# A subject-dependent matrix product with residual: two rows of a sample per partition, and the array in four 64x64 tiles

## The chip, the cores and the metric

The kernel runs on one core of a Trainium2 chip. A core has a matrix engine (TensorE, PE in the profile, with its weight loads as PEld), a vector engine (VectorE, DVE), a scalar engine (ScalarE, ACT), GpSimd (POOL) and SyncE (SP). Here ACT and SP only issue transfers and POOL mostly waits on semaphores for the others. Transfers between the device memory (DRAM) and the on-chip memory (SBUF, 128 partitions) run on 16 DMA engines. Products land in PSUM, which has 128 partitions with 8 banks of 512 fp32 numbers each.

The metric is the time of one execution on the device in microseconds (us), lower is better.

## The reference

For each of 128 samples there is a subject number between 0 and 7, and each subject has a 128x128 matrix. The output is the input plus the matrix of the sample's subject, transposed, times the sample:

```python
# x: (128, 128, 1024) fp32, subjects: (128,) int32, weights: (8, 128, 128) fp32
w = weights[subjects]
out = x + jnp.einsum('bct,bcd->bdt', x, w)
```

So 67.11 MB are read, 67.11 MB are written and 0.52 MB of weights are read. Everything is fp32.

## The kernel before

A sample is a matrix of 128 rows (c) by 1024 columns (t). One row lies in one partition: the 1024 numbers of row c, 4 KB, in partition c. Four samples make a slot (2 MB), and SBUF holds twelve slots in `x_all`. There are 32 slots of work (NT), which run through the twelve places in turn.

- ACT issues all loads, one DMA per sample (`load`, through the helper `transfer` at L67). The DRAM side is given as 32 runs of four rows (16 KB), the SBUF side as 128 partitions of 4 KB. From slot 12 on it waits until the place's previous occupant has been stored. Slot 11 waits until the weights are sorted (`s_sort`), because they pass through its place first.
- POOL waits for each slot's landing and passes it on to TensorE (`s_ready`).
- VectorE reads the subject numbers of a slot into registers and copies the four matrices out of `w_all` (`place`, L165) into the small tiles w0 to w3. A signal `s_go` tells TensorE.
- TensorE multiplies (`multiply`, L174): a slot goes in two halves of two samples. Each sample takes two products of a 128x128 matrix with 128x512 columns. The two halves use the two PSUM tensors ps0 and ps1, of four banks each.
- VectorE adds (`add`, L186): it reads a half of 2048 columns from PSUM, adds the input and writes the sum over the input in `x_all`.
- SP stores a slot when its sums are done (`store`, L67). Between slots 8 and 23 it holds stores back until four more slots are done (EARLY, LAST, BEHIND). The last twelve slots are stored two at a time (4 MB), the others singly (2 MB).

At the start the weights come with one DMA on SP's queue (L192). VectorE sorts them into `w_all` with two transposes (L208, L227) and copies (L230), POOL doing four of sixteen copies. TensorE runs three products of zeros (L200) to wake its clock.

The order on each engine is the order of the code. TensorE's and VectorE's parts are loops with one turn per slot; the lists of ACT, SP and POOL are written out in full. The engines meet only through semaphores.

Of the kernel before, what the change touches and what calls it, by code (L numbers as in the profile page):

```python
# [30 lines left out]
G = 2  # L31
H = 2

N = 512

SLOTS = 12

P_SLOTS = 2

BEHIND = 4  # L40
# [4 lines left out]
PAIR = 2  # L45
WHOLE = 6

DMA = 16

SORTED = 18  # L50

IDLE = 3
# [28 lines left out]
def kernel(  # L81
# [10 lines left out]
    NT = B // (G * H)  # L92
# [4 lines left out]

    room = -(nc.sbuf_base + -nc.sbuf_base % 32) % ALIGN
    if room:
        sbuf("room", C, room // 4)  # L100
    x_all = sbuf("x_all", C, SLOTS * H * G * T)
    xs = [
        x_all[:, i * H * G * T : (i + 1) * H * G * T].rearrange("c (q t) -> c q t", t=T)
        for i in range(SLOTS)
    ]
    w_all = sbuf("w_all", C, S, D)
    w_raw, w_mid, w_late = (xs[SLOTS - 1][:, q, :] for q in range(3))
    ws = [sbuf(f"w{i}", C, 1, D) for i in range(H * G)]
    zeros = sbuf("zeros", C, N)
    given, near, wrap = (sbuf(name, 1, B, dtype=I32) for name in ("given", "near", "wrap"))  # L110
    index = sbuf("index", 1, B + H * G, dtype=I32)
    ps = [
        ctx.enter_context(nc.psum_tensor(f"ps{i}", [D, G, T], F32)).ap() for i in range(P_SLOTS)
    ]

    s_given = tc.alloc_semaphore("s_given")
    s_wall = tc.alloc_semaphore("s_wall")
    s_index = tc.alloc_semaphore("s_index")
    s_zeros = tc.alloc_semaphore("s_zeros")
    s_product = tc.alloc_semaphore("s_product")  # L120
    s_added = tc.alloc_semaphore("s_added")

    s_ready = tc.alloc_semaphore("s_ready")
    s_go = tc.alloc_semaphore("s_go")

    s_slot = [tc.alloc_semaphore(f"s_slot{k}") for k in range(SLOTS)]
    s_head = tc.alloc_semaphore("s_head")
    s_sort = tc.alloc_semaphore("s_sort")

    def emptied(i):  # L130
        turns = i // SLOTS
        return DMA * (H * G + 1) * turns - (DMA * G if i >= SLOTS and i % SLOTS == 0 else 0)

    def load(engine, i, q):
        transfer(
            nc,
            engine,
            xs[i % SLOTS][:, q, :],
            x[i * H * G + q].rearrange("(a r) t -> a (r t)", r=ROWS),
        ).then_inc(s_head if i * H * G + q < G else s_slot[i % SLOTS], DMA)  # L140

    def store(i, n):
        at = i % SLOTS * H * G * T
# [19 lines left out]
    def place(h, subject):  # L163
        for q in range(h * G, (h + 1) * G):
            copy = nc.vector.tensor_copy(ws[q], w_all[:, bass.ds(subject[q], 1), :])  # L165
        copy.then_inc(s_go, 1)
# [143 lines left out]
```

## Time and profile before

| what | value |
|---|---|
| time, median of 3 runs | 322.95 us (322.77 to 322.99) |
| span of the profiled execution, first to last instruction | 320.9 us |
| TensorE matmul busy | 248.9 us (78%) |
| VectorE busy | 172.6 us (54%) |
| bytes moved | 134.76 MB, mean 420 GB/s |
| mean granted TensorE clock | 0.893 of full |

The median of the runs stands 2.05 us above the profiled execution's span: the time of a run also has what lies before the first and behind the last instruction. The profile is of one such execution; no separate run time is given for it.

How to read it: the page cuts the span into 40 equal slices of 8.0 us, and a digit is the busy share of a slice in tenths. In a row of a group, after the bar, stand the busy time in us, the mean duration of one instruction in ns, the idle time of the engine just before them and what ended most of it. A row of a stretch (a:b) has its length, the busy us of PE, PEld, DVE and POOL with the count of instructions, the granted clock, the busy share of the DMA engines and GB/s. A row of the timeline has start, duration (us), engine, line, operation and, in brackets, the idle time before it. A row of a queue has its packets, its MB and its share of the 16 engines' time. The rows of the DMA issues have the size of one and the median time from issue to landing.

### The profile page before, as it was taken

What the parts mean: (1) busy time and instruction counts of PE and PEld (TensorE: products, weight loads), DVE (VectorE), ACT (ScalarE), POOL (GpSimd) and SP (SyncE); (2) the same over time, 40 slices, a digit from 0 to 9 for tenths busy, and PEclk for the clock granted to TensorE, in tenths of its full rate; (3) what the DMA queues carried; (4) which work ended last, traced back from release to release, by engine and by line L of the source; (5) the groups of instructions that cost most, each with busy time, mean ns of one, the idle gap of its engine ahead of it and who ended that gap; (6) DMA issues with size and microseconds to landing.
All of it is one profiled execution on the core that took longest, in us unless ns stands there. A gap on an engine that the chain in (4) does not pass through costs nothing. (4 is left out here: it accounts for less than half of the span.)

```text
span 320.9 us, 2386 instructions
## 1 busy us (share of the span) xinstructions
PE 248.9 (78%) x518; PEld 102.8 (32%) x518; DVE 172.6 (54%) x216; POOL 1.9 (1%) x8
## 2 busy tenths in 40 slices
PE   6199999999997699998498469988599957874000
PEld 2134444444433244443133224333244422331000
DVE  4636776777676167775435362675367745066000
POOL 0200000000000000000000000000000000000000
PEclk9679999999999599999789797999799989599555
DMA  7999999999999999999999999999999999999996
GB/s 294 425 425 412 426 423 432 429 423 425 425 425 425 425 424 425 425 429 425 429 435 431 427 427 429 425 425 425 425 425 425 425 425 425 427 427 455 429 445 274
DMA packets 10803, 134.76 MB, mean 420 GB/s; under 512 B 2481, under 2 KB 2482, under 8 KB 3122
## 3 DMA queue, kind: packets, MB, share of 16 engines
q1 hardware_dynamic: 4658, 67.64, 49.7%
q10 hardware_dynamic: 6144, 67.12, 49.6%
q14 instruction: 1, 0.01, 0.0%
HBM read 67.63 MB, written 67.11 MB: 420 GB/s over the span
## 5 line engine op out<-in xcount | busy, mean ns | idle before, releaser
L174 PE MATMUL ps<-x_all,w 128*128 x512 | 243.8, 635 | 42.0 <-PEq L170 34.3
L186 DVE TENSOR_TENSOR x_all<-ps,x_all 128x2048 f32 x64 | 146.7, 2292 | 117.3 <-DVEq L185 117.3
L174 PEld LDWEIGHTS ps<-x_all,w 128*128 128x128 f32 x512 | 100.9, 203 | 185.2 <-issue 184.6
L165 DVE COPY w<-w_all 128x128 f32 x132 | 23.2, 219 | 0.8 <-DVE w_all L230 0.8
L200 PE MATMUL ps<-zeros 128*128 128x512 f32 x6 | 5.2, 1033 | 1.7 <-DVE zeros L197 1.7
L230 DVE COPY w_all<-x_all 32x256 f32<-32x256 f32 x12 | 3.9, 326 | 0.4
L208 DVE STREAM_TRANSPOSE x_all<-x_all 128x1024 f32<-128x1024 f32 x1 | 2.0, 1992 | 3.1 <-DMA x_all<-in_L_cond_weights_dram 3.1
L200 PEld LDWEIGHTS ps<-zeros 128*128 128x128 f32 x6 | 1.8, 328 | 3.7 <-issue 2.1
L230 POOL COPY w_all<-x_all 32x256 f32<-32x256 f32 x4 | 1.7, 425 | 8.3 <-DVE x_all L227 8.1
L227 DVE STREAM_TRANSPOSE x_all<-x_all 128x1024 f32<-128x1024 f32 x1 | 1.2, 1225 | 0.0
L197 DVE MEMSET zeros<- 128x512 f32 x1 | 0.5, 485 | 1.0 <-SPq L190 1.0
L217 DVE CUSTOM_DVE_ANT_0 index<-near,wrap 1x256 uint16<-1x256 uint16 x1 | 0.3, 280 | 0.0
L215 DVE TENSOR_SCALAR wrap<-near 1x128 int32<-1x128 int32 x1 | 0.2, 215 | 0.0
L213 DVE TENSOR_SCALAR near<-given 1x128 int32<-1x128 int32 x1 | 0.2, 205 | 0.0
L297 POOL MEMSET const-bfloat16-1.0<- 128x1 bf16 x1 | 0.1, 100 | 0.0
L297 POOL MEMSET const-float32-0.0<- 128x1 f32 x1 | 0.1, 98 | 0.2 <-issue 0.2
L297 POOL MEMSET const-uint8-127<- 128x1 uint8 x1 | 0.1, 98 | 0.0
L297 POOL MEMSET const-float32-1.0<- 128x1 f32 x1 | 0.1, 97 | 0.0
L297 DVE BASE_LOAD x1 | 0.0, 21 | 0.1
L211 DVE MEMSET index<- 1x4 int32 x1 | 0.1, 62 | 0.0
## 6 DMA issues: line engine op xcount, KB each, us to landing
x_all<-in_x_dram ACTq DMA_DIRECT2D x128, 512.0 KB, 34.2
out_dram<-x_all SPq DMA_DIRECT2D x20, 2048.0 KB, 18.3
out_dram<-x_all SPq DMA_DIRECT2D x6, 4096.0 KB, 30.3
x_all<-in_L_cond_weights_dram SPq DMA_DIRECT2D x1, 512.0 KB, 3.7
given<-in_itok_B_dram SPq DMA_DIRECT2D x1, 0.5 KB
```

Of the source, the lines that this page charges most:

```text
L165: copy = nc.vector.tensor_copy(ws[q], w_all[:, bass.ds(subject[q], 1), :])
L174: mm = nc.tensor.matmul(ps[h][:, q % G, t : t + N], ws[q][:, 0, :], x_all[:, bass.ds(at, N)], start=True, stop=True,)
L186: nc.vector.tensor_tensor(mine, ps[h].rearrange("d g t -> d (g t)"), mine, ALU.add).then_inc(s_added, 1)
L197: nc.vector.memset(zeros, 0.0).then_inc(s_zeros, 1)
L200: nc.tensor.matmul(ps[P_SLOTS - 1][:, G - 1, :N], zeros[:, :D], zeros, start=True, stop=True)
L208: nc.vector.transpose(w_mid.rearrange("p (e h w j) -> p j h e w", e=S, h=4, w=4), w_raw).then_inc(s_sort, 1)
L213: nc.vector.tensor_scalar(near, given, -S, S - 1, ALU.max, ALU.min).then_inc(s_index, 1)
L215: nc.vector.tensor_scalar(wrap, near, 0, S, ALU.is_lt, ALU.mult).then_inc(s_index, 1)
L217: nc.vector.tensor_tensor(index[:, :B], near, wrap, ALU.add).then_inc(s_index, 1)
L227: nc.vector.transpose(w_late, w_mid).then_inc(s_sort, 1)
L230: engine.tensor_copy(w_all[32 * v : 32 * (v + 1), 2 * o : 2 * (o + 1), :], w_late[32 * o : 32 * (o + 1)].rearrange("c (e v d) -> c v e d", ...
L297: nc = _bacc.Bacc("TRN2", target_bir_lowering=False, num_devices=1)
```

## The change

The layout. A partition now holds two consecutive rows of a sample, 8 KB in one piece, so a sample fills 64 partitions and two samples lie above each other. A slot is still four samples: two pairs, p = 0 from the first half of the batch and p = 1 from the second half (FAR = 64 samples further on). In a pair, h = 0 is the sample in the lower 64 partitions and h = 1 the one in the upper. Inputs and outputs have places of their own: `x_in` for four slots, `x_out` for eight.

The product. The 128 rows of a sample are two rows (r) in each of 64 partitions, and so are the 128 rows of the result (e). So a sample's matrix is cut into four 64x64 pieces (r, e), and a product of 512 columns takes two matmuls (r = 0, 1) that add up in PSUM. Each uses a quarter of the array: rows by h, columns by the output's side. For p = 0 the output lies on the side of the input; for p = 1 it changes sides (`h ^ p`). The four products (p, h) that follow each other in the code use the four different quarters.

The upper sample of p = 1 is multiplied one slot after the slot in which it was loaded (`i - p * h`). With that, the two outputs of p = 1 in a slot are neighbours in the batch, in the order in which they lie, and one DMA of 128 partitions stores the slot. The last sample of the batch is loaded early and fills the gap in slot 0.

The residual. VectorE no longer adds the input: `place` adds the identity (`same`, made by POOL) to the matrix while copying it, so the product is already the sum. VectorE copies PSUM to `x_out` in pieces of 1024 columns. A slot fills all of PSUM in two halves of two banks in each tensor; `s_free` gives a half back to TensorE after its copies. The small weight tiles are double (w00, w01 and w10, w11), filled two slots ahead.

The queues. ACT's list, before and after; 64x8x256 are the weights, 64x2048 a single sample:

```order
L67 DMA x_all<-in_x_dram 128x1024 x44
L67 DMA x_all<-in_x_dram 128x1024 [waits s_sort]
L67 DMA x_all<-in_x_dram 128x1024 x3
L67 DMA x_all<-in_x_dram 128x1024 [waits s_slot0]
L67 DMA x_all<-in_x_dram 128x1024 x3
L67 DMA x_all<-in_x_dram 128x1024 [waits s_slot1]
```

```order
L65 DMA x_out<-in_L_cond_weights_dram 64x8x256
L65 DMA x_in<-in_x_dram 128x2048 x2
L65 DMA x_in<-in_x_dram 64x2048
L65 DMA x_in<-in_x_dram 128x2048 x5
L65 DMA x_in<-in_x_dram 128x2048 [waits s_eaten] x56
L65 DMA x_in<-in_x_dram 64x2048 [waits s_eaten]
```

The weights stand ahead of the samples now, a load is two samples, and the first load that waits is the eighth of two samples where it was the forty-fifth of one.

TensorE's turn of the loop, before (one slot; ps0 and ps1 are the halves of PSUM, w0 to w3 the matrices of the four samples):

```order
L174 ISA [waits s_go,s_ready]
L174 MATMUL ps0<-x_all,w0 128x512
L174 ISA
L174 MATMUL ps0<-x_all,w0 128x512
L174 ISA
L174 MATMUL ps0<-x_all,w1 128x512
```

and after, the first half of a slot (there are four slots in a turn now; the quarters are not shown, w00 belongs to p = 0 and w01 to p = 1):

```order
L210 MATMUL ps0<-x_in,w00 64x512 [waits s_go,s_ready,s_free]
L210 MATMUL ps0<-x_in,w00 64x512
L210 MATMUL ps1<-x_in,w01 64x512 x2
L210 MATMUL ps0<-x_in,w00 64x512 x2
L210 MATMUL ps1<-x_in,w01 64x512 x2
L210 MATMUL ps0<-x_in,w00 64x512 [waits s_free]
```

Eight products of the whole array have become 32 of a quarter, without register work between them, and TensorE waits for a half of PSUM twice per slot.

VectorE's turn, before (half a turn):

```order
L154 TENSOR_LOAD index
L186 ISA [waits s_product]
L186 TENSOR_TENSOR x_all<-ps0,x_all 128x2048
L165 ISA
L165 COPY w0<-w_all 128x128
L165 ISA
L165 COPY w1<-w_all 128x128
```

and after (one slot but for the last three of its four weight tiles):

```order
L222 ISA [waits s_room,s_product]
L222 COPY x_out<-ps0 128x1024
L222 ISA
L222 COPY x_out<-ps1 128x1024
L222 ISA [waits s_product]
L222 COPY x_out<-ps0 128x1024
L222 ISA
L222 COPY x_out<-ps1 128x1024
L186 ISA
L186 TENSOR_TENSOR w00<-w_all,same 64x256
```

The two adds per slot have become four copies, and the plain copies of weights have become adds with the identity.

The core of the diff:

```diff
-SLOTS = 12
-P_SLOTS = 2
-BEHIND = 4
+IN = 4
+OUT = 8
+BEHIND = 3
-IDLE = 3
+IDLE = 8
...
     def load(i, p, first, n):
+        at = (i % IN * P + p) * SIZE
+        low = first % H * A
+        return transfer(
             nc,
+            nc.scalar,
+            x_in[low : low + n * A, at : at + SIZE],
+            x[first : first + n].rearrange("h (b r) t -> (h b) (r t)", r=ROWS),
+        )
...
     def store(i):
+        at = i % OUT * P * SIZE
+        rows = out.rearrange("b (a r) t -> (b a) (r t)", r=R)
+        (step, _), last = rows.ap
         return transfer(
             nc,
             nc.sync,
+            bass.AP(
+                tensor=rows.tensor,
+                offset=rows.offset + H * i * A * step,
+                ap=[[step, C], [(FAR - 1) * A * step, P], last],
+            ),
+            x_out[:, at : at + P * SIZE].rearrange("a (o f) -> a o f", o=1),
+        )
...
-    def place(h, subject):
-        for q in range(h * G, (h + 1) * G):
-            copy = nc.vector.tensor_copy(ws[q], w_all[:, bass.ds(subject[q], 1), :])
-        copy.then_inc(s_go, 1)
+    def place(u, subject):
+        return [
+            nc.vector.tensor_tensor(
+                ws[u][p][h * A : (h + 1) * A],
+                w_all[h * A : (h + 1) * A, bass.ds(subject[p * H + (h ^ p)], 1), :],
+                same[h * A : (h + 1) * A],
+                ALU.add,
+            )
+            for p in range(P)
+            for h in range(H)
+        ]
...
+    def multiply(i):
         nc.tensor.wait_ge(s_go, 1).then_inc(s_go, -1)
         nc.tensor.wait_ge(s_ready, 1).then_inc(s_ready, -1)
+        for b in range(BANKS):
+            if b < BANKS // 2:
+                nc.tensor.wait_ge(s_free, 1).then_inc(s_free, -1)
+            for r in range(R):
+                for p in range(P):
+                    for h in range(H):
+                        bank = b * 2 % BANKS + (b * 2 // BANKS + h) % 2
+                        e, t = divmod(bank * N, T)
+                        rows = slice(h * A, (h + 1) * A)
+                        cols = slice((h ^ p) * A, ((h ^ p) + 1) * A)
+                        at = ((i - p * h) % IN * P + p) * SIZE + r * T + t
+                        mm = nc.tensor.matmul(
+                            ps[p][cols, bank],
+                            ws[i % 2][p][rows, 0, r * D + e * A : r * D + (e + 1) * A],
+                            x_in[rows, at : at + N],
+                            start=r == 0,
+                            stop=r == R - 1,
+                        )
+            if b >= BANKS // 2:
+                mm.then_inc(s_product, 1)
+
+    def copy(slot, p, half):
+        at = slot * (P * SIZE) + (p * SIZE + half * T)
+        return nc.vector.tensor_copy(
+            x_out[:, bass.ds(at, T)],
+            ps[p][:, half * (T // N) : (half + 1) * (T // N)].rearrange("d b n -> d (b n)"),
+        )
+
+    def sort(h):
+        nc.vector.tensor_copy(
+            w_all[h * A : (h + 1) * A].rearrange("c s (r e a) -> c (s r) e a", r=R, e=R),
+            w_raw.rearrange("c (g a e) -> c g e a", a=D // R, e=R),
+        ).then_inc(s_sort, 1)
...
+        for i in range(NT):
+            for p in range(P):
+                if i >= IN - p:
+                    nc.scalar.wait_ge(s_eaten, i - IN + 1 + p)
+                n = H if (i, p) != (NT - 1, 1) else 1
+                load(i, p, p * FAR + i * H, n).then_inc(s_in[i % IN], DMA)
+            if i == 0:
+                load(IN - 1, 1, B - 1, 1).then_inc(s_head, DMA)
...
+        nc.gpsimd.wait_ge(s_head, DMA)
         for i in range(NT):
+            if i >= OUT:
+                nc.gpsimd.wait_ge(s_out[i % OUT], stored(i - OUT)).then_inc(s_room, 1)
+            nc.gpsimd.wait_ge(s_in[i % IN], DMA * P * (i // IN + 1)).then_inc(s_ready, 1)
+
+        for i in range(NT - 1):
+            nc.sync.wait_ge(s_added, i + 1 + (BEHIND if EARLY <= i < NT - LAST else 0))
...
+        with nc.vector.Fori(0, NT // 2) as turn:
+            for u in range(2):
+                subject = subjects_of(bass.ds(turn * (2 * Q) + (u + 2) * Q, Q))
+                slot = (turn * 2 + u) % OUT
+                nc.vector.wait_ge(s_room, 1).then_inc(s_room, -1)
+                for half in range(2):
+                    nc.vector.wait_ge(s_product, 1).then_inc(s_product, -1)
+                    for p in range(P):
+                        copied = copy(slot, p, half)
+                        if half and not p:
+                            copied.then_inc(s_eaten, 1)
+                    copied.then_inc(s_free, 1)
+                placed = place(u, subject)
+                placed[0].then_inc(s_added, 1)
+                placed[-1].then_inc(s_go, 1)
+        with nc.tensor.Fori(0, NT // IN):
+            for i in range(IN):
+                multiply(i)
```

204 lines of the change are left out of this document (93 added, 111 removed).

## The prediction, made before the changed kernel ran

> **What bounds the kernel now.** I read the page from the top: span, busy shares, the 40 slices, the DMA queues.
>
> ```profile
> span 320.9 us, 2386 instructions
> PE 248.9 (78%) x518; PEld 102.8 (32%) x518; DVE 172.6 (54%) x216; POOL 1.9 (1%) x8
> PEclk9679999999999599999789797999799989599555
> DMA  7999999999999999999999999999999999999996
> GB/s 294 425 425 412 426 423 432 429 423 425 425 425 425 425 424 425 425 429 425 429 435 431 427 427 429 425 425 425 425 425 425 425 425 425 427 427 455 429 445 274
> DMA packets 10803, 134.76 MB, mean 420 GB/s; under 512 B 2481, under 2 KB 2482, under 8 KB 3122
> q1 hardware_dynamic: 4658, 67.64, 49.7%
> q10 hardware_dynamic: 6144, 67.12, 49.6%
> ```
>
> No compute engine is above 78%, while the DMA row stands at 9 in 38 of 40 slices and the two queues fill 99.3% of the 16 engines' time. Then I asked for long stretches, so that the edges of large transfers matter little.
>
> ```profile
> 10.00:30.00 20.00, 15.46 (x30) 6.56 (x31) 9.96 (x20) 0.40 (x1) 0.75 1.02 430
> 70.00:118.00 48.00, 42.98 (x92) 17.91 (x92) 29.15 (x34) 0.00 (x0) 0.93 1.01 426
> 133.00:240.00 107.00, 86.21 (x179) 35.64 (x178) 57.00 (x69) 0.00 (x0) 0.92 1.01 426
> 297.00:319.00 22.00, 0.00 (x0) 0.00 (x0) 0.00 (x0) 0.00 (x0) 0.50 0.96 410
> ```
>
> The rate is 426 GB/s, whatever PE does beside it, also in the last 22 us, where only stores run. 134.76 MB at 426 GB/s is 316.3 us, and 4.6 us are left for the first and last slice. So the bound is the transfers. The waits say the same from the other side: VectorE waits for products, and TensorE, in its longest waits (L170 waits for a slot's landing), for data.
>
> ```profile
> DVE x_all L186 <- DVEq L185: 117.3, 64, 8.3
> PE ps L174 <- PEq L170: 34.3, 12, 4.6
> ```
>
> Early on the loads are far ahead, and there the compute shows its own pace. This is VectorE's timeline, one add in two:
>
> ```profile
> 24.63 2.29 DVE L186 TENSOR_TENSOR x_all<-ps,x_all 128x2048 f32 x1 [0.80 <-DVEq L185]
> ...
> 31.69 2.29 DVE L186 TENSOR_TENSOR x_all<-ps,x_all 128x2048 f32 x1 [0.80 <-DVEq L185]
> ...
> 38.74 2.29 DVE L186 TENSOR_TENSOR x_all<-ps,x_all 128x2048 f32 x1 [0.81 <-DVEq L185]
> ```
>
> A slot of four samples takes 7.05 us of compute, and 4.19 MB at 426 GB/s is 9.85 us of transfer. The slack is 2.8 us per slot; the change spends most of it.
>
> The runs' median of 322.95 us is 2.05 us above this execution's span; I carry these 2.05 us over unchanged.
>
> **TensorE, per slot.** The line of the product, and two rows of its weight loads, at half and at full clock:
>
> ```profile
> L174 PEld LDWEIGHTS ps<-x_all,w x512: 186/190/338, 14.5 to 291.6; 128*128 128x128 f32 x171
> L174 PE MATMUL ps<-x_all,w x512: 592/592/1217, 14.5 to 292.0; 128*128 x171
> L174 PEldq FUSED_REGOPS  x256: 46/46/103, 14.4 to 287.3; - x128
> 109.02 0.34 PEld L174 LDWEIGHTS ps<-x_all,w 128*128 128x128 f32 x1 [0.52 <-issue]
> 113.60 0.19 PEld L174 LDWEIGHTS ps<-x_all,w 128*128 128x128 f32 x1 [0.24 <-issue]
> ```
>
> 256 products of the program are 512 matmuls, each with its own weight load: an fp32 product is two instructions. At full clock one follows another every 0.19 + 0.24 = 0.43 us, at half clock every 0.86; a slot is 16 x 0.43 = 6.9 us. After the change a slot has 32 products, 64 instructions, still of 512 columns. If four run at once, 64 / 4 x 0.43 = 6.9 us, as before; if two, 13.8; if none, 27.5. No row shows a quarter of the array at work, so these are the bounds. I take four: the four products that stand next to each other differ in rows or columns of the array, and each pair of r and bank fills it. This choice decides the forecast.
>
> The weight loads, 64 per slot with 64 columns instead of 16 with 128, lie beside the matmuls now. If their time goes with the columns it is 64 x 0.095 = 6.1 us and stays under 6.9; if a load costs 0.19 whatever its width, 12.2 us.
>
> **VectorE, per slot.**
>
> ```profile
> L186 DVE TENSOR_TENSOR x_all<-ps,x_all 128x2048 f32 x64 | 146.7, 2292 | 117.3 <-DVEq L185 117.3
> L165 DVE COPY w<-w_all 128x128 f32 x132 | 23.2, 219 | 0.8 <-DVE w_all L230 0.8
> L230 DVE COPY w_all<-x_all 32x256 f32<-32x256 f32 x12 | 3.9, 326 | 0.4
> L227 DVE STREAM_TRANSPOSE x_all<-x_all 128x1024 f32<-128x1024 f32 x1 | 1.2, 1225 | 0.0
> ```
>
> Removed are two adds (4.6 us) and four copies of weights (0.9). Added are four copies of 1024 columns out of PSUM and four adds of the identity, 64x256. Between 128 columns (219 ns) and 2048 (2292) one column costs 1.08 ns, so a copy is 1.19 us (upper end 1.23, the row of 1024 columns), and an adding of 256 columns 0.36 us (0.33 to 0.45). Together 4.8 + 1.4 = 6.2 us, against 5.5 before.
>
> **The ring of the two.** All of PSUM now belongs to one slot, in two halves. From the end of the third quarter of the matmuls, VectorE copies half 0 (2.4 us, beside the fourth quarter of 1.7) and then half 1 (2.4); only then may the next slot's second quarter start, and two quarters (3.45) bring it to the same point: 8.3 us, with three handoffs 8.3 to 8.8. I take 8.5: above the old 7.05, below the 9.85 of transfer. What hides it is the transfer; from 11.3 us (below) 32 slots and some 10 us for the last copies and store fit into 320 us up to 9.3 us per slot.
>
> **The transfers.** Bytes are the same, and packets of 16 KB too. The loads go from 128 to 65 DMAs, the stores from 26 to 34. q10 with 6144 packets took 49.6 / 67.12 = 0.739% per MB, q1 with fewer packets per MB 0.735%; by that difference (0.2 engine-us per MB for 23 packets) a small packet costs about 9 ns, and 55 fewer DMAs of 16 such packets save 880 x 9 / 16 = 0.5 us. In SBUF and on the way out the contiguous piece is 8 KB instead of 4 KB, 16384 fewer pieces. Their price stands in no row: at least 0, at most that of a packet, 9 ns, which is 9.4 us. The nearest rows are the rates: 426 in the long stretches, 430 over 10 to 30 us. I take 430 as reachable, 134.76 MB x (1/0.426 - 1/0.430) = 2.9 us less; ends 0 and 6.5 (435, the highest slice before 250 us).
>
> The Trainium skill, DMA: Bandwidth & Descriptors (section Why small descriptors are slow), puts a fixed 3 cycles of 32 bytes on each piece, under a ceiling of 435 GB/s: as an estimate, 128/131 of it is 425 GB/s for 4 KB, which the slices agree with, and 256/259 is 430 for 8 KB; by it the sum would lose 3.7 us here.
>
> **The start.** Before:
>
> ```profile
> L200 PE MATMUL ps<-zeros 128*128 128x512 f32 x6 | 5.2, 1033 | 1.7 <-DVE zeros L197 1.7
> x_all<-in_L_cond_weights_dram SPq DMA_DIRECT2D x1, 512.0 KB, 3.7
> 0.90 23.58 ACTq L67 DMA_DIRECT2D x_all<-in_x_dram  x31
> 8.52 4.26 DVE L230 COPY w_all<-x_all 32x256 f32<-32x256 f32 x12
> 13.63 0.63 DVE L165 COPY w<-w_all 128x128 f32 x4 [0.85 <-DVE w_all L230]
> 14.54 9.84 PE L174 MATMUL ps<-x_all,w 128*128 x16 [7.71 <-DVE w L165]
> ```
>
> Both transposes and sixteen sorting copies go; two copies of 2048 columns come (1.8 us each, by 0.84 ns per column between the rows of 128 and 256). Weights at about 5, register load 0.85, sorting 3.7, placing 1.5: 11 us. The sixteen warm-up instructions end there too (six at 0.86 from 1.7, the rest at 0.43: 11.1). So the first slot starts near 11.3 instead of 14.5, and frees its input after 6.9 of matmul and the third copy, at 20.2. But only four input slots exist where twelve did: without a freed slot ACT can issue 8.4 MB, and from 2.5 us (what the first slice lacks) at 426 GB/s these last until 22.2. ACT's wait on a freed slot holds all later loads behind it. Cover: 2 us, about what a transfer needs to get going (the weights' 3.7 less 1.2 of moving). I charge 0.5 us; ends 0 and 4. The weights move from SP's queue to the head of ACT's, so the first samples come 0.52 MB / 426 GB/s = 1.2 us later; no byte is added, and 11.3 already has them. Their 1 KB pieces, 384 more at 9 ns on 16 engines, add 0.2. POOL's new wait (a slot is ready only when the store of eight slots earlier has landed) holds TensorE back; a store is issued three slots after its sum, so it has four slots, 34 us at 8.5, to land, against a median of 18.3 us for the same 2 MB before:
>
> ```profile
> out_dram<-x_all SPq DMA_DIRECT2D x20, 2048.0 KB, 18.3
> ```
>
> I cost it at nothing; a landing above 34 us would make it part of the starved case. The end costs nothing either: three slots of stores are held back (BEHIND) and one is under way, 4 x 4.9 us of transfer, longer than the 11 us that the last slot needs after its load.
>
> **Sum:** 322.95 - 0.5 - 2.9 + 0.2 + 0.5 = 320.2 us.
>
> **Rivals.**
> *Two at once (slower).* Place: TensorE's queue. The two instructions of one product want the same quarter of the array. If a matmul may not start before the one ahead of it in the program has, the second holds up the other three products, and the pattern settles at two at work: 13.8 us per slot. It decides from 9.3 us per slot, or 0.58 us for each four. Time: 11.3 + 32 x 13.8 + 10 + 2 = 465 us. For it: the two-for-one rows above; against: nothing measured. The Trainium skill, TensorE: Matmul & The Clock Gate (section Part 3), states that matmuls begin and end in program order and only weight loads are pulled ahead; no run here shows it for quarters yet.
> *Another limit on TensorE (slower).* Weight loads of 0.19 in a row: 11.3 + 32 x 12.2 + 12 = 414 us; or quarters not overlapping at all, about 900.
> *Starved (slower).* The ring at 9.6 instead of 8.5, or the start's gap at its far end with stores held back from slot 8 on while four input slots are full: 11.3 + 32 x 9.6 + 12 = 331; 324 to 340.
> *No faster pieces (the same).* The rate stays 426: 322.95 - 0.5 + 0.2 + 0.5 = 323.2.
>
> **Chances.** What a measurement of this kernel can tell from no change is about 0.2%, 0.65 us. Forecast 0.42, two at once 0.30, another TensorE limit 0.12, starved 0.10, the same 0.06. So faster 0.42, same 0.06, slower 0.52: the likeliest single case is faster, though the slower ones together weigh more. Its own range is 316.5 (rate 435, the rest unchanged) to 322.3. For 8 in 10 the range must take in the two-at-once case: 316.5 to 470.
>
> **What would show it.** Right: the slices at 428 to 431 GB/s in long stretches, matmuls of four quarters starting within a fraction of 0.43 us, VectorE's copies at 1.2 us, first product near 11.3, no slice near 22 us below 9. Two at once: PE at 9 in every slice, full clock throughout, DMA near 300 GB/s, and matmul starts in pairs each 0.43 us. Starved: DMA digits of 7 or 8 between 20 and 120 us. Wrong altogether, if PSUM copies take well over 1.23 us or the identity's adding over 0.45, for then the ring passes 9.3 without TensorE.

## The result, and the profile after

The changed kernel takes 338.05 us (median of four runs, 336.89 to 341.25) beside 322.86 us for the kernel before on the same chip: a ratio of 1.049, 95% interval 1.044 to 1.054. The prediction was 320.2 us, faster. It is 15 us slower. All times below are medians of undisturbed runs; one run of the kernel with half of the products, 332.36 us at a lower granted clock, is not counted.

This is the page of the changed kernel: the span, the busy times, the 40 slices (8.4 us each now) and the transfers.

```profile
span 336.2 us, 5241 instructions
PE 251.0 (75%) x2064; PEld 93.3 (28%) x2064; DVE 209.0 (62%) x275; POOL 1.0 (0%) x6
DMA  7998999999999968999999999999999999999993
GB/s 224 368 404 273 354 417 431 433 433 427 429 431 431 413 277 281 433 429 429 429 433 431 431 429 427 433 431 429 431 427 429 431 431 431 428 400 427 429 433 157
DMA packets 10440, 134.81 MB, mean 401 GB/s; under 512 B 1602, under 2 KB 2115, under 8 KB 2115
```

TensorE is as busy as before (251.0 against 248.9 us), although it now runs 2048 matmul instructions of a quarter of the array each. Away from the holes most slices move 427 to 433 GB/s, where before most moved 425; there are 879 fewer packets under 512 B. Most of the time is lost in three holes of the GB/s row: the first five slices (0 to 4), slices 14 and 15 (277 and 281), and the last one, 39 (157). The same by stretches (GB/s is the last column):

```profile
0.00:10.00 10.00, 8.33 (x13) 3.56 (x14) 4.47 (x12) 1.05 (x6) 1.00 0.77 261
10.00:20.00 10.00, 6.93 (x44) 2.44 (x46) 3.00 (x8) 0.00 (x0) 0.83 1.00 370
14.00:17.00 3.00, 2.48 (x12) 0.88 (x16) 0.00 (x0) 0.00 (x0) 0.50 0.97 415
20.00:30.00 10.00, 8.54 (x80) 3.08 (x76) 6.30 (x8) 0.00 (x0) 1.00 0.84 334
25.00:26.00 1.00, 1.00 (x12) 0.16 (x4) 1.00 (x2) 0.00 (x0) 1.00 0.04 16
30.00:50.00 20.00, 16.39 (x147) 5.68 (x136) 14.71 (x18) 0.00 (x0) 1.00 0.99 367
70.00:100.00 30.00, 22.14 (x200) 8.63 (x204) 20.61 (x29) 0.00 (x0) 1.00 1.01 431
100.00:150.00 50.00, 41.01 (x367) 15.07 (x359) 32.71 (x42) 0.00 (x0) 1.00 0.92 377
150.00:200.00 50.00, 39.78 (x344) 14.52 (x344) 36.58 (x48) 0.00 (x0) 0.98 1.01 430
320.00:336.00 16.00, 0.00 (x0) 0.00 (x0) 2.36 (x5) 0.00 (x0) 0.53 0.69 293
```

and the answering stretches of the kernel before:

```profile
0.00:10.00 10.00, 5.16 (x6) 1.85 (x6) 5.60 (x12) 1.50 (x7) 0.99 0.80 315
30.00:50.00 20.00, 20.00 (x47) 8.41 (x46) 14.20 (x19) 0.00 (x0) 1.00 1.00 415
310.00:320.90 10.90, 0.00 (x0) 0.00 (x0) 0.00 (x0) 0.00 (x0) 0.50 0.79 337
```

A stretch of length t at g GB/s loses t x (1 - g/430) against full flow. After the change that makes 3.9 + 1.4 + 2.2 + 2.9 = 10.5 us up to 50 us, 6.2 us between 100 and 150, and 5.1 us behind 320. Before it was (against 426) 2.6 + 0.5 = 3.1 at the start, nothing in the middle and 2.3 at the end. So the holes cost 7.4 + 6.2 + 2.8 = 16.4 us, and the higher rate gives 2.9 back (134.8 MB at 430 instead of 426). That is 13.5 of the 15.3 us between the two spans; the rest is spread over single slices.

The engines' own work came out much as costed. These are the groups of the products, the copies and the adding of the identity (mean ns of one behind the busy time), then rows of the timeline: the start, one slot of TensorE with one of its bursts of weight loads, and VectorE's turns early on.

```profile
L210 PE MATMUL ps<-x_in,w 64*64 64x512 f32 x2048 | 241.2, 615 | 64.8 <-PEq L201 58.1
L222 DVE COPY x_out<-ps 128x1024 f32 x128 | 147.8, 1217 | 104.9 <-DVEq L323 104.9
L186 DVE TENSOR_TENSOR w<-w_all,same 64x256 f32<-64x256 f32 x136 | 57.1, 420 | 3.1
...
x_out<-in_L_cond_weights_dram ACTq DMA_DIRECT2D x1, 512.0 KB, 6.1
```

```profile
7.02 2.47 DVE L228 COPY w_all<-x_out 64x2048 f32<-64x2048 f32 x2 [3.60 <-DMA x_out<-in_L_cond_weights_dram]
9.64 3.50 DVE L186 TENSOR_TENSOR w<-w_all,same 64x256 f32<-64x256 f32 x8
14.52 8.43 PE L210 MATMUL ps<-x_in,w 64*64 64x512 f32 x64 [3.07 <-PEq L201]
...
108.01 7.10 PE L210 MATMUL ps<-x_in,w 64*64 64x512 f32 x64 [3.25 <-DVE x_out L222]
108.47 0.18 PEld L210 LDWEIGHTS ps<-x_in,w 64*64 64x64 f32 x4 [0.25 <-issue]
...
21.59 4.62 DVE L222 COPY x_out<-ps 128x1024 f32 x4 [8.44 <-DVEq L323]
30.35 4.62 DVE L222 COPY x_out<-ps 128x1024 f32 x4 [2.37 <-DVEq L323]
39.12 4.62 DVE L222 COPY x_out<-ps 128x1024 f32 x4 [2.38 <-DVEq L323]
```

Four quarters do work at once: 64 matmuls take 7.10 us, and in the trace the four of a group start within 0.05 us of each other. The ring of TensorE and VectorE turns every 8.76 us (21.59, 30.35, 39.12), below the 9.75 us that 4.19 MB take at 430 GB/s. What is short in the holes is transfers that may start. From 25.06 us (the third copy of slot 0, 21.59 + 3 x 1.16) a new load may start only when a place of `x_in` is freed, one slot (2.1 MB) per turn: 239 GB/s at 8.76 us. While stores are held back, little more than that flows (277 and 281).

Idle DMA engines are not the whole loss. The column before GB/s, the busy share of the DMA engines, stands at 1.01 in a full stretch and at 0.84 from 20 to 30 us and 0.99 from 30 to 50: by it some 2 of the 5.2 us lost there are idle engines, and some 4.5 of the 6.2 us between 100 and 150 (0.92). In the rest the engines were busy with packets that took longer: the loads' packets of 16 KB took 1.05 us each between 31 and 32 us, where 0.61 is usual. Why they are slow after the bus has nearly stood still is not shown. Where it never stood still, in the run with eight input places below, the same 30 us ran at 428 GB/s.

### The profile page after: what moved, and what is told of

It reads as the page before. It is cut to its first block, busy times and chain, and to the rows that moved or that the text cites. A ratio compares the mean times of both kernels' runs of the same rounds, so it can differ in the third digit from the quotient of the medians.

```text
span 336.2 us, 5241 instructions
## 1 busy us (share of the span) xinstructions
PE 251.0 (75%) x2064; PEld 93.3 (28%) x2064; DVE 209.0 (62%) x275; POOL 1.0 (0%) x6
## 5 line engine op out<-in xcount | busy, mean ns | idle before, releaser
L210 PE MATMUL ps<-x_in,w 64*64 64x512 f32 x2048 | 241.2, 615 | 64.8 <-PEq L201 58.1
L222 DVE COPY x_out<-ps 128x1024 f32 x128 | 147.8, 1217 | 104.9 <-DVEq L323 104.9
L210 PEld LDWEIGHTS ps<-x_in,w 64*64 64x64 f32 x2048 | 89.3, 137 | 216.6 <-issue 216.6
L186 DVE TENSOR_TENSOR w<-w_all,same 64x256 f32<-64x256 f32 x136 | 57.1, 420 | 3.1
L246 PE MATMUL ps<-x_out 128*128 128x512 f32 x16 | 9.8, 781 | 1.7 <-DVE x_out L243 1.7
L246 PEld LDWEIGHTS ps<-x_out 128*128 128x128 f32 x16 | 3.9, 254 | 6.7 <-issue 5.0
L228 DVE COPY w_all<-x_out 64x2048 f32<-64x2048 f32 x2 | 2.4, 1220 | 3.6 <-DMA x_out<-in_L_cond_weights_dram 3.6
L273 DVE TENSOR_SCALAR x_out<-x_out 1x128 int32<-1x128 int32 x1 | 0.2, 215 | 0.6 <-DMA x_out<-in_itok_B_dram 0.6
L275 DVE TENSOR_SCALAR x_out<-x_out 1x128 int32<-1x128 int32 x1 | 0.5, 461 | 0.0
## 6 DMA issues: line engine op xcount, KB each, us to landing
out_dram<-x_out SPq DMA_DIRECT2D x31, 2048.0 KB, 17.7
out_dram<-x_out SPq DMA_DIRECT2D x2, 512.0 KB, 12.7
```

The costliest lines, as they stand in the source:

```text
L186: nc.vector.tensor_tensor(ws[u][p][h * A : (h + 1) * A], w_all[h * A : (h + 1) * A, bass.ds(subject[p * H + (h ^ p)], 1), :], same[h * A : ...
L210: mm = nc.tensor.matmul(ps[p][cols, bank], ws[i % 2][p][rows, 0, r * D + e * A : r * D + (e + 1) * A], x_in[rows, at : at + N], start=r == ...
L222: return nc.vector.tensor_copy(x_out[:, bass.ds(at, T)], ps[p][:, half * (T // N) : (half + 1) * (T // N)].rearrange("d b n -> d (b n)"),)
L228: nc.vector.tensor_copy(w_all[h * A : (h + 1) * A].rearrange("c s (r e a) -> c (s r) e a", r=R, e=R), w_raw.rearrange("c (g a e) -> c g e ...
L246: nc.tensor.matmul(ps[P - 1][:, BANKS - 1], zeros[:, :D], zeros, start=True, stop=True)
L273: nc.vector.tensor_scalar(near, given, -S, S - 1, ALU.max, ALU.min).then_inc(s_index, 1)
```

## The experiments

The theory after the first reading: input may run only four slots ahead of the sums (at the start not quite that: seven loads of two samples and the single one), where twelve common places let it run up to twelve ahead before. Whenever one direction of transfer pauses (at the start, with nothing to store yet; from slot 8 on, with stores held back), the other cannot take its time. The rivals were the hold by itself, the longer ring (8.76 instead of 7.05 us), the start by itself, and, later, a DMA engine that runs late.

**Dropping the hold (BEHIND).**

```diff
-BEHIND = 3
+BEHIND = 0
```

> Stores are no longer held back from slot 8 on (BEHIND 0 for 3), nothing else. Theory A (four input slots are too few: the DMA engines run dry when the loads may not go on and no store is due): the trough between 118 and 134 us, 377 GB/s over 100 to 150 us, goes, which is 6.2 us; with less stores kept for the end up to 3 us come back there: 332 to 335 us. Theory B (the ring of TensorE and VectorE, 8.76 us per slot, sets the time): no change, 337 to 339. Theory C (the start alone: transfers to 64 partitions, small pieces): no change either.

Measured: 338.01 us (336.92 to 338.84), ratio 1.047 (1.045 to 1.049). The slices:

```profile
GB/s 223 364 418 342 378 428 426 434 430 434 422 434 430 432 422 434 430 430 424 432 430 432 424 434 428 432 424 434 428 432 426 432 432 428 422 406 366 258 196 251
```

The hole in the middle is gone, and the same time is lost in the last five slices, when the loads are through and no store is kept for the wait on the last slots. So the hold only chooses where the time is lost. The gain that theory A expected did not come; 338.01 is the number that theories B and C gave, though not their mechanism, since both expected nothing to change. The start (418, 342, 378 in slices 2 to 4) is some 2 us better than in the profile of the changed kernel, and the edit has no part in that, for it acts from slot 8 on: here TensorE kept its full granted clock in slot 0, whose 64 matmuls took 7.10 us instead of 8.43 (granted clock 0.50 from 14 to 17 us, in the stretches above).

**Eight places in, four out, without the hold.**

```diff
-IN = 4
-OUT = 8
-BEHIND = 3
+IN = 8
+OUT = 4
+BEHIND = 0
```

> Eight input and four output slots in place of four and eight, in the same memory, stores not held back. Theory A: the loads go on to about 41 us without a freed slot, so the trough from 26 to 44 us (about 5 us) and that at 118 to 134 us (6.2 us) both go: 325 to 330 us. Theory B: no change, 337 to 339, since the ring stays 8.76. Theory C: the slow first 14 us stay, the rest too: above 334.

Measured: 336.98 us (335.62 to 338.23), ratio 1.042 (1.039 to 1.044).

```profile
GB/s 214 351 431 423 429 430 434 425 429 429 429 432 431 429 429 429 432 431 432 425 429 432 434 429 427 432 429 434 427 427 432 429 431 430 429 386 384 55 216 250
```

From the third slice on the start is full: with eight places for the input its hole from 26 us on does not exist. Four places for the output keep nothing for the end, and it runs dry there (55 GB/s). Both needs want the same memory. Theory A's 325 to 330 us failed, since it counted the two holes that go and not the one that opens at the end.

**The weights on SP's queue, beside the first samples.**

```diff
         transfer(
             nc,
-            nc.scalar,
+            nc.sync,
             w_raw.rearrange("a (s f) -> a s f", s=S),
```

> The weights' transfer (64 partitions, 1 KB pieces) goes back to SP's queue, beside the first samples instead of ahead of them. Theory A: the first product comes up to 2 us earlier, the time falls by 0 to 2 us: 336 to 338. Theory B: the same. Theory C: the rate in the first 14 us rises from about 300 to over 400 GB/s and 4 us or more are saved: 334 or less.

Measured: 352.5 us (352.2 to 356.1), ratio 1.095 (1.089 to 1.101), and every theory missed it. The DMA issues' row of the weights, two stretches and the first product:

```profile
x_out<-in_L_cond_weights_dram SPq DMA_DIRECT2D x1, 512.0 KB, 21.5
...
10.00:25.00 15.00, 1.26 (x3) 0.19 (x1) 3.36 (x8) 0.00 (x0) 0.62 0.99 357
27.00:40.00 13.00, 11.23 (x88) 3.87 (x92) 6.89 (x10) 0.00 (x0) 0.86 0.05 10
...
27.32 3.52 PE L210 MATMUL ps<-x_in,w 64*64 64x512 f32 x16 [16.06 <-DVE w L186]
```

The weights land 21.5 us after their issue instead of 6.1, the first product starts at 27.3, all four places are full, and for 13 us the DMA engines do next to nothing (10 GB/s). The four places turn a late start of the products into an idle bus, about one for one: the first product is 12.8 us later, the kernel 14.5 us longer. The Trainium skill, DMA: Bandwidth & Descriptors (section Queues, rings and completion order), says that a DMA engine takes turns between its queues packet by packet. The trace agrees, with turns of about one piece: from 6 to 20 us it has 323 pieces of 1 KB and 278 packets of 16 KB. As an estimate, of 512 pieces each engine has 32, and if each waits for one 16 KB packet of the other queue (0.61 us) and takes 0.05 us itself, they take 32 x 0.66 = 21 us.

**Half of the products (a faster ring).** Only r = 0 is multiplied (the expectation names r = 1; the work is the same), so half of each sum is left out.

```diff
-            for r in range(R):
+            for r in range(1):
...
-                            stop=r == R - 1,
+                            stop=True,
```

> Leaves out half of the product: only r = 1 is multiplied (64 of 128 rows of the contraction), so that a quarter of a slot's matmuls takes 0.86 us and the ring falls from 8.76 to about 7.0 us per slot, that of the kernel before. Buffers and transfers are as in the changed kernel. Theory A (depth): the trough at 118 us is filled by what the faster ring has issued by then (8 slots x 1.7 us), the one near 26 us shrinks by 2 to 3 us: 328 to 332, still slower than before. Theory B (ring): all of the loss goes, 320 to 323. Theory C: 337 to 339.

Measured: 327.5 us (326.9 to 328.7), ratio 1.015 (1.011 to 1.018).

```profile
GB/s 221 358 431 433 424 433 431 425 437 431 427 433 427 427 374 404 429 433 429 429 435 431 431 429 429 433 427 431 433 429 431 431 431 431 428 408 410 427 431 192
```

With TensorE's share halved the ring turns every 7.04 us, the hole of the start from 26 us on is gone and the one in the middle (374, 404) is about a quarter of its size. A faster ring frees input earlier, so the split of the memory costs less; 4 us over the kernel before remain. It came out 0.5 us below the first theory's range; the theories of the ring alone (320 to 323) and of the start alone (337 to 339) are well off.

**No change of sides (two quarters instead of four).** The pair p = 1 keeps its sides, so its outputs are on the wrong halves, and only two quarters of the array are in use.

```diff
-                        cols = slice((h ^ p) * A, ((h ^ p) + 1) * A)
+                        cols = slice(h * A, (h + 1) * A)
```

> The samples of p = 1 keep their side (columns of the array by h instead of h ^ p), so a slot uses two of the four quarters of the array; half of the outputs land on the wrong side. It settles what the fourfold use is worth. If the two instructions of a product hold up the products behind them only on their own quarter (what the trace of the changed kernel says: four matmuls start within 0.05 us), the matmuls of a slot take 13.8 us and the time is about 14.5 + 32 x 14 + 12 = 470 to 480 us. If TensorE works on two at once anyway, as the rival said, no change: 338.

Measured: 469.6 us (469.55 to 469.66), ratio 1.455 (1.452 to 1.458).

```profile
span 467.9 us, 5241 instructions
PE 451.0 (96%) x2064; PEld 158.6 (34%) x2064; DVE 211.9 (45%) x275; POOL 1.0 (0%) x6
```

PE is at 96%: with two quarters the products are the bound, at the price that the prediction gave its rival "Two at once" (465 us). Changing sides is what makes four.

**Input freed earlier.** VectorE's queue signals that a place of the input is free as soon as the last product of the slot is done, instead of after the third copy.

```diff
                 for half in range(2):
+                    if half:
+                        nc.vector.wait_ge(s_product, 1).then_inc(s_eaten, 1)
                     nc.vector.wait_ge(s_product, 1).then_inc(s_product, -1)
                     for p in range(P):
                         copied = copy(slot, p, half)
-                        if half and not p:
-                            copied.then_inc(s_eaten, 1)
```

> The input slot is given back when TensorE's last matmul is done, instead of behind VectorE's third copy; about 3.5 us earlier per slot, the ring stays 8.76. Theory S (the split of the memory: with four input slots the loads can neither run ahead at the start nor use the time in which stores are held back): the trough at 26 us goes (3 to 4 us), that at 118 us shrinks: 332 to 335. Theory R (the ring of 8.76 us against 7.05 is what costs): 337 to 339.

Measured: 334.28 us (332.32 to 335.82), ratio 1.037 (1.034 to 1.041).

```profile
GB/s 224 359 430 415 398 425 430 434 426 430 430 432 428 404 242 381 420 420 430 434 422 438 430 428 430 424 436 424 436 424 434 424 428 432 427 416 412 428 438 181
```

The start's slices 2 to 4 go from 404, 273, 354 to 430, 415, 398; most of the middle's hole stays (384 GB/s over 100 to 150 us, after 377). The time falls by 3.8 us. The edit frees a place 2.1 us earlier, not the 3.5 expected: ACT issues the next loads at 21.29 and 30.06 us, in the run without the hold, whose start has the same full clock, at 23.39 and 32.16. In the profile of the changed kernel it was 25.11, so the two profiles differ at the start by more than the edit, and how much of the 3.8 us is the clock's was not measured.

**The kernel before, with the lead of the changed one.** Its loads may be at most four slots ahead of the sums; all else, the twelve places and 4 KB pieces too, is as before.

```diff
+            if i >= 4:
+                nc.scalar.wait_ge(s_added, (i - 3) * H)
```

> The kernel before, with one wait more: a load may be at most four slots ahead of the sums, as with four input slots; the ring stays 7.05 and the pieces 4 KB. Theory S: a trough near 25 us, one where the stores are held back (slots 8 to 12), or stores missing at the end: 328 to 334. Theory R: 323 to 324.

Measured: 331.06 us (330.19 to 334.74), ratio 1.029 (1.022 to 1.035).

```profile
GB/s 303 428 353 246 415 422 418 442 416 434 424 416 442 418 410 338 345 430 424 426 430 420 432 426 424 432 418 426 430 428 430 420 424 432 426 430 446 418 426 307
```

One wait in the old kernel makes the same two holes in nearly the same places: slices 2 and 3 (353, 246) and 15 and 16 (338, 345). It costs 8.2 us, against 15.2 for the whole change. This is the strongest of the runs, since nothing else of the change is in it.

**The kernel before, with the ring of the changed one.** Each half is given one more product of the first sample's columns, which TensorE then does twice. The expectation was 8.77 us per slot; VectorE's adds show 8.58 (60.59, 69.17, 77.75).

```diff
-        for q in range(h * G, (h + 1) * G):
-            for t in range(0, T, N):
+        for q, t in [(h * G, 0)] + [(q, t) for q in range(h * G, (h + 1) * G) for t in range(0, T, N)]:
+            if True:
```

> The kernel before, with one product more (the first of each half is done twice), so that a slot takes 8.77 us of TensorE instead of 7.05, as the ring of the changed kernel; buffers as before. Theory R: the loss appears here too, 331 to 337. Theory S: twelve common slots hide it, 323 to 325.

Measured: 323.32 us (323.17 to 323.73), ratio 1.0016 (1.0007 to 1.0026). The slower ring alone costs half a microsecond when the input may run twelve slots ahead. With a lead of four the ring does count, as the run with half of the products shows.

**Hold back gradually, free early, and the last sample on SP's queue.** The stores fall back one slot more every five slots instead of three at once, and the last sample's load moves beside the weights. The edit of the early freed input is in it too and not shown again.

```diff
+        load(IN - 1, 1, B - 1, 1, nc.sync).then_inc(s_head, DMA)
...
-            if i == 0:
-                load(IN - 1, 1, B - 1, 1).then_inc(s_head, DMA)
...
-            nc.sync.wait_ge(s_added, i + 1 + (BEHIND if EARLY <= i < NT - LAST else 0))
+            nc.sync.wait_ge(s_added, i + 1 + (min(BEHIND, max(0, i - 3) // 5) if i < NT - LAST else 0))
```

> The early-freed input of the run before, and in addition: the stores are held back one slot more every five slots (one from slot 8, two from 13, three from 18, none from 24) instead of three at once at slot 8; and the load of the last sample's 64 partitions goes on SP's queue beside the weights, which lie on the other 64 partitions. The base is that run's 334.3 us. Theory 'the loads cannot use a sudden pause of the stores': at a ring of 8.76 us the loads can take 2.1 MB per 8.76 us, 239 of 430 GB/s, so the stores fall behind by one slot in about 44 us, five slots, and a hold that grows so costs nothing. The hole of the run before in slices 15 and 16 (242 and 381 GB/s of 430 in 8.26 us each, 4.6 us) goes, and the start gains 0 to 2.4 us: 327 to 330, no slice below 415 between 40 and 290 us, and no new hole after 295. Rival 'conserved': what is not lost in the middle comes back at the end, as when the hold was dropped: 332 to 335, with slices below 380 after 290 us.

Measured: 328.91 us (327.38 to 331.78), ratio 1.017 (1.013 to 1.020). Slices, and the end by microseconds:

```profile
GB/s 179 423 435 351 350 435 425 431 429 433 427 429 431 431 431 429 433 427 433 427 431 425 431 429 433 429 421 429 429 433 431 433 425 433 418 419 425 431 405 43
...
321.00:322.00 1.00, 0.00 (x0) 0.00 (x0) 0.00 (x0) 0.00 (x0) 0.50 0.85 360
322.00:323.00 1.00, 0.00 (x0) 0.00 (x0) 0.00 (x0) 0.00 (x0) 0.50 0.23 98
323.00:324.00 1.00, 0.00 (x0) 0.00 (x0) 0.00 (x0) 0.00 (x0) 0.50 0.08 33
327.00:328.00 1.00, 0.00 (x0) 0.00 (x0) 0.00 (x0) 0.00 (x0) 0.50 0.08 33
```

The middle is whole, and no five slices at the end run dry: a hold that grows at the pace at which the ring can give the loads more than half of the bus costs nothing there. The time came out as expected, the gain at the start did not: slices 3 and 4 are holes again (351, 350). With that goes a first slot at half clock once more (8.79 us); whether it is the cause was not tested. And from 323 to 328 us the DMA share is 0.07 to 0.08 in each microsecond: one of sixteen engines (0.0625) is still at work while the others are done. The trace's packets show it: from 323.0 us on nine of 16 KB follow one another, 0.61 us each, with no other store packet beside them.

**The same, with ScalarE copying half of PSUM.** ScalarE copies the p = 1 halves and VectorE the p = 0 halves; the loads are issued by ScalarE between its two copies.

```diff
-                    for p in range(P):
-                        copied = copy(slot, p, half)
-                    copied.then_inc(s_free, 1)
+                    copy(slot, 0, half).then_inc(s_free, 1)
...
+                done = nc.scalar.wait_ge(s_product1, 2 * i + half + 1)
+                if half:
+                    done.then_inc(s_done1, 1)
+                    nc.scalar.wait_ge(s_eaten, i + 1)
+                    if i + IN - 1 < NT:
+                        feed(i + IN - 1, 1)
+                    if i + IN < NT:
+                        feed(i + IN, 0)
+                nc.scalar.copy(
+                    x_out[:, at + half * T : at + (half + 1) * T],
+                    ps[1][:, half * (T // N) : (half + 1) * (T // N)].rearrange("d b n -> d (b n)"),
+                ).then_inc(s_copied1, 1)
```

> The kernel with the growing hold, and ScalarE copies the halves of PSUM of the second row of samples while VectorE copies the first (it issues the freed loads between its two copies). The halves are then free 1.2 us after their products, inside the next quarter of the matmuls (1.7 us), so the ring falls from 8.76 to the 64 matmuls' own 6.9 to 7.1 us. Theory 'lead and ring': with 7.0 us a slot computes 2.7 us faster than its 9.75 us of transfer, four input slots suffice after the start, and what remains against the kernel before is the first 20 us (2 to 4 us) against the gain in rate (3.3 us): 320 to 324 us. Rival 'ScalarE becomes the ring': its copy takes over 1.7 us, or the issuing of two loads per slot delays its second copy past the next quarter; then the ring stays at 8 us or more and the time at 326 to 330.

Measured: 331.27 us (329.59 to 331.54), ratio 1.024 (1.022 to 1.026), so not faster than the run before it; the theory's 320 to 324 us failed. ScalarE's copies, and the issuing of the two loads ahead of its second one:

```profile
L293 ACT COPY x_out<-ps 128x1024 f32<-128x1024 f32 x64 | 64.8, 1012 | 224.5 <-PE ps L217 166.5
...
161.36 1.13 ACTq L65 DMA_DIRECT2D x_in<-in_x_dram  x2
162.53 1.01 ACT L293 COPY x_out<-ps 128x1024 f32<-128x1024 f32 x1 [1.89 <-issue]
163.73 7.43 PE L217 MATMUL ps<-x_in,w 64*64 64x512 f32 x64 [0.48 <-PEq L208]
171.89 0.66 PE L217 MATMUL ps<-x_in,w 64*64 64x512 f32 x4 [0.72 <-PEq L208]
```

A copy takes 1.01 us, but issuing two loads takes 1.13 us first, so the ring here only falls to 8.16 us (163.73 to 171.89). The rival named this place, though its 326 to 330 us was passed too. The run before it had already filled the bus from 41 us on, so a faster ring had little to win there; why it is 2 us slower was not followed up.

**The weights in pieces of 8 KB.** Is the late engine made by the 512 pieces of 1 KB? The bytes are the same, but the partitions hold other elements of the weights, so the products are of other numbers. Once in the changed kernel, once in the one with the gradual hold:

```diff
-            w_raw.rearrange("a (s f) -> a s f", s=S),
-            weights.rearrange("s (a r) d -> a s (r d)", r=R),
+            w_raw,
+            weights.rearrange("s (k r) d -> (s k) (r d)", k=A // S),
```

> The changed kernel with one edit: its 512 KB of weights come as 64 contiguous pieces of 8 KB instead of 512 pieces of 1 KB (so the partitions hold other elements of the weights than the products want; instructions and bytes are the same). In the last 4 us of the changed kernel's profile the DMA share is 0.10, 0.08, 0.04, 0.04, where one of sixteen engines alone is 0.0625: one engine is some 3 us behind the other fifteen. Theory 'a late engine from the start': that engine falls behind among the 1 KB pieces, each load is complete only when it is, and with four input slots the others wait for it. Then the tail after 331 us goes, and 2 to 4 us of the start's trough with it: 331 to 335 us against 338.0. Rival 'the lead alone': the pieces do not matter beyond their own transfer, of which at most 2 us are saved before the first product, and the troughs stay: 336 to 338.5, with a tail of one engine as before.

> The kernel with the early-freed input and the growing hold (328.9 us), with the same edit of the weights' pieces. In its profile one engine worked alone from 323 to 328 us, and slices 4 and 5 of 40 were at 351 and 350 GB/s. By the theory of the late engine both go: 5 us at the end and up to 3 at the start, 320 to 324 us, beside 323 for the kernel before. By the rival it stays within 1 us of where it was: 327.5 to 329.5.

Measured: 338.10 us (337.31 to 339.07), ratio 1.047 (1.045 to 1.049); and 329.54 us (327.36 to 330.89), ratio 1.019 (1.016 to 1.022). Both are where they were without the edit, and one engine still ends alone (a DMA share of 0.04 to 0.11 from 323 to 328 us in the second). The theory of the late engine from the weights falls. The trace of the changed kernel, which has a landing per engine for each load, shows when an engine falls behind: the last of the sixteen landings trails the one before it by 0.3 us near 130 us, 1.0 near 190, 1.7 near 233 and 5.2 near 300. The ground is lost little by little in the second half, not at the start. Why stays open.

No version of the changed kernel that computes everything beat the kernel before. The best, with the gradual hold, is 1.7% slower.

## Why the prediction was wrong, point by point

- **The bound and the rate: right.** "I take 430 as reachable": long stretches run at 430 to 431. The estimate of 430 GB/s for 8 KB pieces, which the prediction worked out from the Trainium skill, DMA: Bandwidth & Descriptors (section Why small descriptors are slow), agrees with the trace. That is 2.9 us won, as charged. Three slips beside it change nothing: "also in the last 22 us" stands over a row that reads 410 GB/s and not 426, 16384 pieces at 9 ns on 16 engines are 9.2 us and not 9.4, and the rate of 435 gives 316.7 us and not 316.5.
- **Four at once: right.** 64 matmuls in 7.10 us (6.9 forecast), 469.6 us without the change of sides. "Two at once" (0.30) and "Another TensorE limit" (0.12) did not happen: four weight loads of 64 columns take 0.18 us together. The rule of the Trainium skill, TensorE: Matmul & The Clock Gate (section Part 3), that matmuls stay in program order need not be given up: the two instructions of each fp32 product did not hold the other quarters up.
- **VectorE and the ring: right, at the upper end.** The copy took 1217 ns (1.19 to 1.23 forecast), the adding of the identity 420 ns (0.36, upper end 0.45), the ring 8.76 us (8.3 to 8.8, taken 8.5). That "what hides it is the transfer" holds for twelve common places (+0.5 us at 8.58 us per slot) and not for four.
- **The start: the step that failed first.** It was charged with 0.5 us, ends 0 and 4, on a cover of 2 us: input freed at 20.2, loads lasting until 22.2. Measured: the first product at 14.52 instead of 11.3, and the input freed at 25.06. The weights landed at 7.0 instead of 5, the sorting took 2.47 us instead of 3.7, and the weight tiles of slot 0 lay ready at 11.4 (half of the 3.50 us from 9.64 on): there two errors nearly cancelled, which is luck. What the prediction put at nothing ("11.3 already has them") is TensorE's wait for the samples, which come in slices of 224 and 368 GB/s. By the landings in the trace those of slot 0 were in at 12.7 us and the single last sample, for which POOL waits before it passes on any slot, at 14.2. So 3.2 of the 4.9 us come from the later first product; another 1.3 come from the clock, which was granted at 0.50 from 14 to 17 us after that wait, so that the slot took 8.43 us instead of 7.10. (The wait alone does not decide this: in the run without the hold it was as long, 3.25 us, and the clock stayed full.) The same slow beginning made the four slots last until 25, so the cover was nil and the bus nearly stood for a microsecond (16 GB/s). The price was taken to be that gap alone, but the flow stays short until 50 us. It measured 7.4 us: 2.7 before 20 us, and 4.7 behind.
- **The hold and the end: the second failed step.** "The end costs nothing either: three slots of stores are held back" counted what the hold gives at the end and not what it takes at slot 8: 6.2 us, because loads at 239 GB/s cannot fill the bus while three stores pause. Without the hold the same time is lost at the end, so what the hold was to cover was not free either. At the end 2.8 us more are lost, most of them to one late engine (from 331 to 335 us, below).
- **The waits on POOL: right, as far as the profile shows.** A store landed after 17.7 us (median), against the 34 us allowed, and all of VectorE's 104.9 us of idle time before its copies ended with a product (L323), none with a free place of the output (L321).
- **The rival "Starved"** (324 to 340 us, chance 0.10) is what happened, by its second form and nearly with its mark: DMA digits of 8, 6 and 8 in slices 3, 14 and 15. Its mechanism was written down with the right place and then held to be unlikely. In the kernel before, the hold of four slots left no hole; the run of that kernel with a lead of four shows that it was free only because twelve places let the loads run on.
- **The range.** 316.5 to 470 holds 338 by luck: it was stretched so far for "Two at once", which did not happen. The forecast's own range ended at 322.3.

## What to carry to other kernels

When one pool of buffers is split into places for input and places for output, ask for each pause of one direction how long the other can go on with the places it has, at the pace at which compute frees them. A slower ring that costs next to nothing with a deep common pool (0.5 us here) costs much with a shallow split (10.5 us here, by the run with half of the products), and a hold on stores that left no hole before took 6 us in the middle of the run. If stores have to be kept for the end, let the hold grow with the loads' surplus rather than start at once; the run that did so also had two other edits, but its middle shows no hole.

## What the runs showed that was not expected

- One of the sixteen DMA engines can end 2.5 to 5.5 us after the others, and with it the kernel (3.5 here). The last microseconds of the changed kernel:

```profile
330.00:331.00 1.00, 0.00 (x0) 0.00 (x0) 0.00 (x0) 0.00 (x0) 0.50 0.58 246
331.00:332.00 1.00, 0.00 (x0) 0.00 (x0) 0.00 (x0) 0.00 (x0) 0.50 0.10 41
334.00:335.00 1.00, 0.00 (x0) 0.00 (x0) 0.00 (x0) 0.00 (x0) 0.50 0.04 16
```

  The kernel before, and its version with a lead of four, end without this, and so do the two runs with BEHIND at 0, which run dry at the end (0.7 us). What makes one engine late was not found.
- A small transfer beside large ones on another queue is slowed by more than its bytes: 512 KB of 1 KB pieces took 21.5 us instead of 6.1.
- A transfer to 64 partitions is slow: from 11 to 14 us, where the single last sample comes in, the flow was 284 GB/s with the engines 97% busy, and its packets of 16 KB took up to 1.27 us where 0.61 is usual. Moved beside the weights, which lie on the other 64 partitions (the run with the gradual hold), the second 10 us rose from 370 to 436 GB/s, and the first 10 us fell from 261 to 218, so that only some 0.5 us of it remained.

```profile
11.00:14.00 3.00, 0.45 (x2) 0.00 (x0) 2.06 (x5) 0.00 (x0) 0.98 0.97 284
```

```profile
0.00:10.00 10.00, 8.33 (x13) 3.66 (x14) 5.24 (x14) 1.05 (x6) 1.00 0.78 218
10.00:20.00 10.00, 7.90 (x48) 2.98 (x50) 2.21 (x6) 0.00 (x0) 0.83 1.02 436
```
